# Query projections by seven block products in layer 2, an earlier last product with v, and PSUM rings kept by hand

## The chip, the cores and the metric

The kernel runs on one core of a Trainium2 chip. All arithmetic is in fp32. The metric is device time in microseconds (us) from one launch of the whole program; the median of several runs is compared. Separate from those runs, one execution was taken by the hardware profiler, and its records are the profile that is read here.

A word on the names in the profile: PE is TensorE (matmuls), PEld its weight loads, DVE is VectorE, ACT is ScalarE, POOL is GpSimd, SP is SyncE, which only issues DMA transfers here. "SPq", "ACTq" and "POOLq" are the queues on which these engines issue transfers. A line number such as L192 is a line of the kernel's file.

## The reference

The input x holds 4 images of 512 channels and 32x32 pixels, so 1024 positions ("tokens") each. Four residual layers follow one another, each behind a group norm over 32 groups:

```python
x = x + L0(gn(x))   # attention, 8 heads; scores mixed over heads, softmax, instance norm, product with v, projection
x = x + L1(gn(x))   # channel means -> a small simulated quantum circuit -> one gate per channel
x = x + L2(gn(x))   # attention, 8 heads of 64 channels
x = x + L3(gn(x))   # 2048 memory items: scores, the 8 best, softmax over them, weighted sum of the items
```

The change is mostly in layer 2:

```python
q = conv1x1(x, Wq, bq)                       # 512x512 weights on 512x1024
k, v = conv1x1(x, Wkv, bkv)                  # two more of the same size
attn = softmax(einsum('bhct,bhcs->bhts', q, k) * SCALE)      # SCALE = 1/8
out = conv1x1(einsum('bhts,bhcs->bhct', attn, v), Wp, bp)
```

## The kernel before, in words

Channels lie on the 128 partitions in KC = 4 chunks, tokens along the free dimension in two halves of NB = 512. A full 1x1 convolution is 32 matmuls of 128x512, and each fp32 matmul is two records in the profile. [...]the kernel uses three *pairs* of banks as a ring (`pairs`) and two single banks (`pv_bank`, `pt_bank`).

**Order.** TensorE executes in program order, and `pin` (L56) keeps the order in which the program writes the instructions for all that are wrapped in it. So the order of the work is written out by hand: a loop calls generators a step at a time, and each step issues a few instructions for several engines. Instructions without `pin` are placed by the framework's scheduler.

**Head.** `first()` (L294) loads image 0 in four chunks and the weights `w_q` in four chunks, alternately, on SP's queue; the parameter vectors (`gamma`, `beta`, `bproj` ...) are loaded before it on ACT's queue. For every chunk, DVE takes statistics (`stats`, L308), two tiny matmuls with `gavg` and a chain on POOL, ACT and DVE make the group's mean and deviation (`means`, `deviations`), DVE scales the chunk (`normalize`, L324), and `multiply` (L330) adds the chunk's share of the first q projection. The completion of a DMA is counted by one of eight counters, used in turn; an instruction that would reuse a counter waits until the transfer before it on this counter is complete.

**Layers 0 and 1.** For each image b = 0..3, `step` (L1436) runs for 32 units and 7 more (`STEPS` = 32, `LAG` = 7), in which the tail of this image's attention stands beside the q projections of the next image (`piece`, in the last seven steps given the list `qs`). `apply` (L523) is the product with v for a unit; after every fourth, `take_out` (L590) lets ACT copy the bank pv to SBUF, and only then may the next `apply` begin to write the bank. After the last image come the first q, k, v projections of layer 2 (`take_q2`, `take_k2`, `take_v2`) and the output projection of layer 0 for the last image (`put_out`, L729), each in a pair whose number is the last argument.

**Layer 2.** Then the PSUM pools are closed and opened again (L1590 to 1595): a pool `ps_s` with three pairs and a pool `ps_m` with two banks, from which tiles are drawn in order. Per image there are 16 units (`UNITS2`): head pair m, half n of the queries, and half of the keys from t0. `scores2` (L1165) computes four score tiles of a unit, ACT takes their exponentials, and inside it `apply2` (L1206) does the product with v of the unit before. POOL and DVE add the exponentials over the keys (L1197 to L1202); `over_keys` (L1229) ends that sum with transposes and reductions on DVE; `invert2` (L1240) makes the sum over partitions with four small matmuls (L1251), copies and inverts it, writes it to DRAM (`r`) and reads it back to all partitions (`rb`) on SP's queue; `finish2` (L1269) multiplies the block of the product with v by it (L1277).

**The borders.** Between two images of layer 2 (after b = 0, 1, 2) the next image's q, k and v and this image's output projection are computed (L1650 to L1675): q in the plain way by `take_q2`, L1141, evacuated by DVE with bias and SCALE (L1145); then the product with v of the last unit; then k, v and, after one `scores2`, the output by `seven` (L1033). That splits both factors in 2x2 blocks and needs seven products of half-size blocks in place of eight: `SEVEN` lists the products and the blocks of the result to which each is set or added. The sums of the blocks of x (t1, t3, t4 and two made in place) come from `input_sums` (L1000) on DVE, 1.2 us each. The sums of the blocks of the weights come from `weight_sums` (L1007), five DVE instructions once per matrix at the first border; the sums in place go to DRAM and are loaded for later images, while three of them stay in SBUF (`places7`). Each product (8 records by channels) fills one pair; ACT or DVE takes it from there, and `behind` is a generator of other work (norm and gating of images) that is advanced a step at a time.

**Layer 3** draws its score tiles from the same pools (`attention`, L1326; `read`, L1400).

Of the kernel before, what the change touches and what calls it, by code (L numbers as in the profile page):

```python
# [41 lines left out]
def fast_net(ctx: ExitStack, tc: tile.TileContext, a: dict, out: bass.AP, flag: bass.AP):  # L42
# [21 lines left out]
    def chan(src, name):  # L64
        t = const.tile([P, KC], F32, tag=name, name=name)
        nc.scalar.dma_start(out=t, in_=src)
        return t

    gamma = const.tile([P, NH], F32, tag="gamma", name="gamma")
    nc.scalar.dma_start(out=gamma, in_=a["in_gamma"].partition_broadcast(P))  # L70
    beta = const.tile([P, NH], F32, tag="beta", name="beta")
    nc.scalar.dma_start(out=beta, in_=a["in_beta"].partition_broadcast(P))
    bproj = chan(a["b_proj"], "bproj")
    bq2 = chan(a["bq"], "bq2")
    bk2 = chan(a["bk"], "bk2")
    bp2 = chan(a["bp"], "bp2")
    fcb = chan(a["fc_b"], "fcb")

    fcw = const.tile([NQ, C], F32, tag="fcw", name="fcw")
    nc.scalar.dma_start(out=fcw, in_=a["fc_w"])  # L80
    qpar = const.tile([P, NL * NQ], F32, tag="qpar", name="qpar")
    nc.scalar.dma_start(out=qpar, in_=a["q_params"].partition_broadcast(P))
# [3 lines left out]
    ident = const.tile([P, P], F32, tag="ident", name="ident")  # L86
    make_identity(nc, ident)
    ones = const.tile([P, P], F32, tag="ones", name="ones")
    nc.gpsimd.memset(ones, 1.0)
# [13 lines left out]
    )  # L103
    NS = 32
# [71 lines left out]
    def place(at, name):  # L176

        return pairs[at % 3] if at is not None else ps_s.tile([P, 2, NB], F32, tag="sc", name=name)
# [115 lines left out]
    def first():  # L294
# [3 lines left out]
        w = I["w_q"] = eight_k([P, KC, C], "w_q0_0", 0)  # L298
        for k in range(KC):
            nc.sync.dma_start(out=xn[:, k, :], in_=x_v[0, :, k, :])  # L300
            nc.sync.dma_start(out=w[:, k, :], in_=a["w_q"][:, k, :])
        I["w_k"] = load_w("w_k", "w_k0_0", 1)
# [5 lines left out]
        def stats(k):  # L308
            mv = small.tile([P, 2], F32, tag="mv0", name=f"mv0_{k}")
            st = small.tile([P, 2, 6], F32, tag="bnst", name=f"st_a0_{k}")  # L310
            for i in range(2):
                pin(nc.vector.bn_stats(st[:, i, :], xn[:, k, i * NB:(i + 1) * NB]))
            pin(nc.vector.bn_aggr(mv, st.rearrange("p i s -> p (i s)")))
            parts[k] = group_coeffs_parts(mv[:, 0:1], mv[:, 1:2], f"a0_{k}")

        def means(k):
            next(parts[k])
            next(parts[k])

        def deviations(k):  # L320
            next(parts[k])
            found[k] = next(parts[k])
# [15 lines left out]
        stats(0)  # L338
        means(0)
        stats(1)  # L340
        deviations(0)
        means(1)
        normalize(0)
        for k in range(KC):
            if k + 2 < KC:
                stats(k + 2)
            multiply(k, 0)
            if k + 1 < KC:
                deviations(k + 1)
            multiply(k, 1)  # L350
            if k + 1 < KC:
                normalize(k + 1)
            if k + 2 < KC:
                means(k + 2)
# [626 lines left out]
    def load2(b):  # L981
        for key in ("Wq", "Wk", "Wv"):
            load_sums(b, key, b == 1 or key == "Wq")

    def load_sums(b, key, plain):
        w = img[b][key] = eight_k([P, KC, C], f"{key}2_{b}")
        nc.sync.dma_start(out=w, in_=a[key] if plain else w_sums[key])

    H = C // 2
    w_sums = {key: dram.tile([P, KC, C], F32, tag=f"ws_{key}", name=f"ws_{key}")  # L990
              for key in ("Wk", "Wv", "Wp")}
# [15 lines left out]
    def weight_sums(b, key):  # L1007

        w = img[b][key]
        a11, a21, a12, a22 = quarters(w, H)  # L1010
        s1, s6, s7 = places7[key]
        add7(s1, a11, a22)
        sub7(s7, a12, a22)
        add7(a12, a11, a12)
        sub7(s6, a21, a11)
        add7(a21, a21, a22)
        nc.sync.dma_start(out=w_sums[key], in_=w)

# [14 lines left out]
    def seven(b, key, src, multiply, view, block, begin, done=None):  # L1033
# [7 lines left out]
        for i, (at, uses) in enumerate(SEVEN):  # L1041
            ps = ps_s.tile([P, 2, NB], F32, tag="sc", name=f"{key}_{b}_{at}")
# [24 lines left out]
    def seven_k(b):  # L1067

        dst = img[b]["k"] = big("k", f"k2_{b}")

        def begin(i, j, ps):
            for m in range(2 * i, 2 * i + 2):
                pin(nc.scalar.activation(
                    dst[:, m, j * NB:(j + 1) * NB], ps[:, m % 2, :],
                    AF.Identity, bias=bk2[:, m:m + 1]))

        return seven(b, "Wk", img[b]["xn"], by_channels, lambda ps: ps,
# [63 lines left out]
    def take_q2(b, m, at=None):  # L1141
        I = img[b]
        if m == 0:
            I["q"] = big("q", f"q2_{b}")
        project(I["Wq"], tokens(I["xn"]), m, at, lambda ps: pin(nc.vector.tensor_scalar(  # L1145
            I["q"][:, m, :], ps, bq2[:, m:m + 1], SCALE, ALU.add, ALU.mult)), f"q2_{b}")
# [18 lines left out]
    def scores2(b, u, before=None):  # L1165
# [8 lines left out]
        def exp2():  # L1174
            e = places2[:, count[0] % 6]
            count[0] += 1
            pin(nc.scalar.activation(e, scs[len(es)], AF.Exp))  # L1177
            es.append(e)

        for i, t in enumerate(range(t0, t0 + 4)):  # L1180
            sc = ps_s.tile([P, 2, NB], F32, tag="sc", name=f"sc_{nm}_{t}")
# [21 lines left out]
        if t0 == TC - 4:  # L1203
            over_keys(b, m, n)

    def apply2(b, u, exp2=None):  # L1206
# [3 lines left out]
        if t0 == 0:  # L1210
            invert2(b)
            I["pv", m, n] = ps_m.tile([P, NB], F32, tag="mm", name=f"pv_c{b}_{m}_{n}")
# [27 lines left out]
    def invert2(b):  # L1240
# [7 lines left out]
        ps = ps_s.tile([P, 2, NB], F32, tag="sc", name=f"rs_{nm}")[:, 0, 0:NS]  # L1248
# [77 lines left out]
    def attention(b, tt, between=None):  # L1326
# [3 lines left out]
        for i, (lo, hi) in enumerate(  # L1330
                ((0, T), (T, T + NB), (T + NB, NI)) if (b, tt) == tiles[-1] else ((0, T), (T, NI))):
            sc = ps_s.tile([P, T], F32, tag="sc", name=f"at_{nm}_{i}")
# [54 lines left out]
    def read_last(b, tt, picked, dg):  # L1387

        got, et, rs, xr = picked
        tp = ps_m.tile([P, KC, P], F32, tag="mm", name=f"stp_{b}_{tt}")  # L1390
# [9 lines left out]
    def read(b, tt, picked):  # L1400
# [9 lines left out]
        tp = ps_m.tile([P, KC, P], F32, tag="mm", name=f"stp_{nm}")  # L1410
# [25 lines left out]
    def step(b, s, mid, piece):  # L1436
# [35 lines left out]
        if tiled:  # L1472
            apply(b, s - LAG)
        if not tiled or s >= STEPS:
# [6 lines left out]
        if tiled and part == 3:  # L1481
# [58 lines left out]
    for b in range(B):  # L1540
# [27 lines left out]
        for m in range(KC):  # L1568
            ks[m](m + 1)
# [9 lines left out]
        if last:  # L1579
# [5 lines left out]
            for i in range(TC // 2):  # L1585
                take_v2(0, i, i + 2)
            for m in range(KC):
                put_out(b, m, m)

    stage.close()  # L1590
    pairs.clear()
    by_scalar.append(True)
    stage = ctx.enter_context(ExitStack())
    ps_s = stage.enter_context(tc.tile_pool(name="ps_s2", bufs=3, space=PSUM))
    ps_m = stage.enter_context(tc.tile_pool(name="ps_m2", bufs=2, space=PSUM))

    def small_ps(name):
        return ps_s.tile([P, 2 * NB], F32, tag="sc", name=name)
# [19 lines left out]
    for i, key in enumerate(("Wk", "Wv", "Wp")):  # L1618
        places7[key] = nine[3 * i:3 * i + 3]
    nc.gpsimd.tensor_scalar_mul(same, same, 8.0 / T)  # L1620
# [3 lines left out]
    for b in range(B):  # L1624
# [6 lines left out]
        for s, u in enumerate(UNITS2):  # L1631
# [4 lines left out]
            if s >= 1:  # L1636
                scores2(b, u, UNITS2[s - 1])
            for _ in range(2):
                if s >= 3 and last:
                    next(behind, None)  # L1640
                if s >= 8:
                    next(ahead, None)
        run_out(ahead)
        if last:
            apply2(b, UNITS2[-1])
# [4 lines left out]
        early, later = input_sums(img[b + 1]["xn"])  # L1650
        for m in range(KC):
            take_q2(b + 1, m)
            if m < 3:
                early[m]()
            if b == 0 and m < 2:
                weight_sums(1, ("Wk", "Wv")[m])
            next(behind, None)
        load_sums(b, "Wp", b == 0)
        apply2(b, UNITS2[-1])
        for i, _ in enumerate(seven_k(b + 1)):  # L1660
            if i == 0:
                invert2(b)
                for fn in later:
                    fn()
            if i == 4 and b == 0:
                weight_sums(0, "Wp")
            next(behind, None)
        finish2(b)
        early, later = input_sums(img[b]["o"])
        for i, _ in enumerate(seven_v(b + 1)):  # L1670
            if 2 <= i < 5:
                early[i - 2]()
            elif i >= 5:
                later[i - 5]()
            next(behind, None)  # L1675
        run_out(behind)
        scores2(b + 1, UNITS2[0])
        seven_out(b)

    def check_range():  # L1680
# [3 lines left out]
        tps = ps_m.tile([P, NB], F32, tag="mm", name="tot")  # L1684
# [748 lines left out]
```

## Time and profile before

| | us |
|---|---|
| median of 3 runs | 2556.93 (2554.43 to 2558.5) |
| the profiled execution | 2558.39 |
| its span, first to last instruction | 2556.6 |

The profiled execution lies 1.79 us over its span, and it is the slowest but one of the four executions.

The stretches that the change touches, each with its busy time in us and the number of instructions in brackets:

| stretch (us from the start) | length | PE busy | DVE busy | ACT busy | POOL busy |
|---|---|---|---|---|---|
| 0 to 20, head | 20.0 | 10.42 (27) | 8.22 | 1.28 | 6.18 |
| 20 to 330, first image of layer 0 | 310.0 | 297.46 (3415) | 200.13 | 146.75 | 140.78 |
| 1262 to 1275, start of layer 2 | 13.0 | 10.68 (43) | 3.24 | 4.91 | 2.78 |
| 1382 to 1500, first border | 118.0 | 115.80 (377) | 76.94 | 16.75 | 20.12 |
| 1606 to 1725, second border | 119.0 | 118.75 (374) | 72.35 | 19.02 | 15.03 |
| 1825 to 1945, third border | 120.0 | 119.75 (378) | 73.33 | 19.88 | 15.16 |

How to read it: a stretch in which PE's busy time equals its length leaves nothing to fetch but the matmuls themselves. What is missing is time in which TensorE stood still. Busy times of different engines overlap and are not to be added.

### The profile page before, as it was taken

The numbers are of one execution on the slowest core, as the hardware profiler recorded it, in microseconds if no ns is written. First come the engines' busy times: TensorE is split into PE (matmuls) and PEld (weight loads), VectorE is DVE, ScalarE is ACT, GpSimd is POOL, SyncE is SP. The second block draws the span as 40 slices with busy tenths as digits, with TensorE's granted clock in tenths as the row PEclk, the third lists the DMA queues.
The fourth block names the chain that finished last, engine by engine and source line by source line (L and its number), as shares of the span: only waits on it lengthen the run. The fifth ranks groups of instructions, "written<-read, shape, count | busy, mean of one in ns | idle before, by whom it ended". The sixth has DMA issues, their size and how long they took to land.

```text
span 2556.6 us, 47828 instructions
## 1 busy us (share of the span) xinstructions
PE 2503.3 (98%) x18534; PEld 1180.8 (46%) x18534; DVE 1685.8 (66%) x2785; ACT 985.8 (39%) x1177; POOL 1192.5 (47%) x1700
## 2 busy tenths in 40 slices
PE   8999999999999999999999999999999999999998
PEld 3344534554355534555633533453353344444445
DVE  4599448872688438881267567576657648788875
ACT  1467336651666336651153145125314612121211
POOL 3266415553465425553074147117405617566655
PEclk9999999999999999999999999999999999999999
DMA  2578438872698428982301130121014046767665
GB/s 83 145 207 237 125 120 226 244 211 74 172 243 235 131 82 211 244 248 101 124 16 55 70 112 18 54 83 59 21 54 148 18 130 190 219 186 217 187 184 170
DMA packets 187211, 361.39 MB, mean 141 GB/s; under 512 B 32729, under 2 KB 96217, under 8 KB 182882
## 3 DMA queue, kind: packets, MB, share of 16 engines
q1 hardware_dynamic: 105744, 178.71, 22.6%
q0 software_dynamic: 49152, 142.79, 20.6%
q10 hardware_dynamic: 32082, 36.76, 5.3%
q8 instruction: 149, 2.44, 0.4%
q14 instruction: 84, 0.69, 0.1%
HBM read 186.96 MB, written 36.96 MB: 88 GB/s over the span
## 4 chain that ended last, share of the span: by engine, by line
PE 74%; issue 10%; POOL 7%; DVE 3%; ACT 3%; DMA 2%; POOLq 0%; SPq 0%; ACTq 0%; DVEq 0%
PE pair L192 10%; PE sc_c L1183 9%; PE pv_c L1220 9%; PE pv L532 8%; POOL got L1360 7%; PE pair L467 6%; PE pair L493 5%; PE pt L425 5%; PE pt L721 4%; PE q L192 3%; PE Wk L1056 3%; PE Wv L1063 3%; ACT e L500 2%; PE Wp L1056 2%; PE at L1335 2%
## 5 line engine op out<-in xcount | busy, mean ns | idle before, releaser
L482 POOL DMA_DIRECT2D s<-ss x512 | 258.2, 511 | 399.5 <-PE pair L493 113.4
L506 DVE STREAM_TRANSPOSE eT<-e 128x1024 f32<-128x1024 f32 x256 | 316.5, 1236 | 193.6 <-ACT e L500 193.0
L1360 POOL DMA_INDIRECT got<-in_mem,ix x256 | 279.5, 1092 | 213.2 <-issue 122.1
L1177 ACT ACTIVATE eT<-sc_c 128x1024 f32<-128x1024 f32 x256 | 248.0, 1022 | 330.7 <-PE sc_c L1183 204.8
L521 DVE BATCH_NORM_STATS2 st<-e 128x6 f32<-128x256 f32 x1024 | 350.7, 404 | 0.0
L500 ACT ACTIVATE e<-pair 128x1024 f32<-128x1024 f32 x256 | 250.7, 1022 | 167.5 <-PE pair L493 137.2
L1201 POOL TENSOR_TENSOR e<-eT 128x1024 f32<-128x1024 f32 x96 | 232.3, 2421 | 168.6 <-DVE out L1125 69.5
L467 PE MATMUL pair<-k,q 64*32 64x512 f32 x4096 | 267.4, 598 | 12.7 <-ACT e L500 12.7
L473 ACT COPY ss<-pair 128x1024 f32<-128x1024 f32 x256 | 247.3, 1020 | 77.5 <-DMA s<-ss 37.9
L532 PE MATMUL pv<-eT,v 128*64 128x128 f32 x4096 | 250.7, 276 | 8.9 <-ACT pv L592 8.9
L532 PEld LDWEIGHTS pv<-eT,v 128*64 128x64 f32 x4096 | 221.1, 137 | 76.7 <-issue 54.5
L1183 PE MATMUL sc_c<-q,k 64*128 64x512 f32 x1024 | 240.9, 607 | 3.1 <-DVE xr L684 2.3
L1220 PE MATMUL pv_c<-eT,v 128*64 128x512 f32 x1024 | 233.0, 597 | 0.0
L1202 DVE TENSOR_TENSOR eT<-eT,e 128x1024 f32<-128x1024 f32 x96 | 136.3, 1420 | 146.3 <-POOL e L1201 146.1
L1197 POOL TENSOR_TENSOR eT<-eT 128x1024 f32<-128x1024 f32 x32 | 77.8, 2433 | 206.8 <-ACT eT L1177 202.8
L1407 DVE SCALAR_TENSOR_TENSOR acc<-got,et,acc 128x512 f32<-128x512 f32 x210 | 157.9, 752 | 7.5
L493 PE MATMUL pair<-s,wmix 32*32 32x512 f32 x4096 | 160.6, 600 | 2.3 <-issue 2.1
L1183 PEld LDWEIGHTS sc_c<-q,k 64*128 64x128 f32 x1024 | 93.6, 187 | 141.0 <-issue 71.9
L1340 ACT COPY att<-at 128x1024 f32<-128x1024 f32 (+1 forms) x65 | 64.9, 999 | 219.7 <-PE at L1335 212.9
L467 PEld LDWEIGHTS pair<-k,q 64*32 64x32 f32 x4096 | 57.0, 105 | 179.9 <-ACT e L500 86.2
L1220 PEld LDWEIGHTS pv_c<-eT,v 128*64 128x64 f32 x1024 | 68.0, 137 | 136.8 <-issue 136.8
L1335 PE MATMUL at<-memT,xn_d 128*128 128x512 f32 x256 | 120.7, 594 | 0.0
(335 smaller groups left out, 3431.3 us busy)
## 6 DMA issues: line engine op xcount, KB each, us to landing
s<-ss SPq DMA_DIRECT2D x512, 128.0 KB
s<-ss POOLq DMA_DIRECT2D x512, 128.0 KB
rb<-r POOLq DMA_DIRECT2D x64, 128.0 KB
o<-o SPq DMA_DIRECT2D x32, 256.0 KB
xr<-in_x ACTq DMA_DIRECT2D x32, 256.0 KB
x<-xr SPq DMA_DIRECT2D x32, 256.0 KB
xr_c<-x SPq DMA_DIRECT2D x32, 256.0 KB
rb_c<-r SPq DMA_DIRECT2D x64, 128.0 KB
```

The source lines that it names most:

```text
L192: pin(nc.tensor.matmul(ps[:, n, :], w[:, k, m * P:(m + 1) * P], rhs(k, n), start=(k == 0), stop=(k == KC - 1),))
L467: pin(nc.tensor.matmul(sc[m * NS:(m + 1) * NS, r, :], q[r * HD:(r + 1) * HD, m, s * NS:(s + 1) * NS], k_[r * HD:(r + 1) * HD, m, n * NB:(n ...
L482: pin(relays[side].dma_start(out=s2[2 * m + r::NH], in_=ss[m * NS:(m + 1) * NS, r, :]))
L493: pin(nc.tensor.matmul(mixed(s, r // 2)[t * NS:(t + 1) * NS, r % 2, :].rearrange("p (qq k) -> p qq k", qq=2), wmix[r * NS:(r + 1) * NS], s ...
L500: pin(nc.scalar.activation(e[:, half].rearrange("p r qq k -> p (r qq k)"), flat2(mixed(s, half)), AF.Exp))
L506: pin(nc.vector.transpose(eT[:, j % 2].rearrange("p b (qq i r) x -> p i r qq b x", qq=2, i=4)[:, i, 2 * half:2 * half + 2], e[:, half].rea ...
L521: pin(nc.vector.bn_stats(st[:, i, 2 * half + r, qq, :], e[:, half, r, qq, :]))
L532: pin(nc.tensor.matmul(pv[r * HD:(r + 1) * HD, gp, :], I["v"][:, t, g * HD:(g + 1) * HD], eT[:, j % 2, t, :, 4 * g:4 * g + 4], start=(t == ...
L1177: pin(nc.scalar.activation(e, scs[len(es)], AF.Exp))
L1183: pin(nc.tensor.matmul(sc[:, r, :], I["k"][r * HD:(r + 1) * HD, m, t * P:(t + 1) * P], I["q"][r * HD:(r + 1) * HD, m, n * NB:(n + 1) * NB] ...
L1220: pin(nc.tensor.matmul(pv[r * HD:(r + 1) * HD, :], I["v"][:, t, h * HD:(h + 1) * HD], e[:, r, :], start=(t == 0), stop=(t == TC - 1),))
L1360: pin(nc.gpsimd.indirect_dma_start(out=got[:, i, :], out_offset=None, in_=a["mem"], in_offset=bass.IndirectOffsetOnAxis(ap=ix[:, i:i + 1], ...
```

## The change

- The parameter loads are collected in a list and issued by `first` after the loads of x and w_q; chunk 0 of x comes in two halves; the chunks' group means move from POOL to DVE; 17 matmuls of ones (128x128) are put before and between the first small matmuls; statistics and scaling of the first chunks change places on DVE.
- In `step`, for the steps beyond `STEPS`, `take_out` comes before `piece`.
- At the start of layer 2 the pools are not reopened. `next_pair` and `next_bank` hand out the three pairs and the two banks in turn; k, v and the output projection at that place use pairs shifted by one or two. In a border, small matmuls use the bank that is idle (`at_border`).
- q at the borders goes by seven products. Its weight sums are made in units 10 to 14 of image 0 and stored; because three of them share a place with those of Wp, they are stored too (`w_more`) and loaded again for later images. SCALE is applied in the exponential. t1 is made in the last unit but one; t4 and t3 before q; `over_keys` of the last unit is called after them (of its DVE instructions only the second reduction ends up behind them).
- The last product with v comes ahead of q; `invert2` of the last heads stands at the fifth product of q, `finish2` at the second product of k, behind the load of Wp.
- `ahead` (statistics and norm for the next image) is advanced from unit 7 on, not 8.

The diff, cut to its core:

```diff
 
-    def chan(src, name):
-        t = const.tile([P, KC], F32, tag=name, name=name)
-        nc.scalar.dma_start(out=t, in_=src)
+    later = []
+
+    def held(shape, name, src):
...
         w = I["w_q"] = eight_k([P, KC, C], "w_q0_0", 0)
+        for n in range(2):
+            nc.sync.dma_start(out=xn[:, 0, n * NB:(n + 1) * NB], in_=x_v[0, :, 0, n * NB:(n + 1) * NB])
         for k in range(KC):
-            nc.sync.dma_start(out=xn[:, k, :], in_=x_v[0, :, k, :])
+            if k > 0:
+                nc.sync.dma_start(out=xn[:, k, :], in_=x_v[0, :, k, :])
             nc.sync.dma_start(out=w[:, k, :], in_=a["w_q"][:, k, :])
+        for load in later:
+            load()
         I["w_k"] = load_w("w_k", "w_k0_0", 1)
...
+            mv = parts[k][0]
+            ps = small_ps(f"gps_a0_{k}")
+            pin(nc.tensor.matmul(ps[:, 0:1], gavg, mv[:, 0:1], start=True, stop=True))
+            dm, sq, gm = (column(name, k) for name in ("dm", "gsq", "gm"))
+            pin(nc.vector.tensor_sub(dm, mv[:, 0:1], ps[:, 0:1]))
+            pin(nc.vector.scalar_tensor_tensor(sq, dm, dm, mv[:, 1:2], ALU.mult, ALU.add))
+            pin(nc.vector.tensor_copy(gm, ps[:, 0:1]))
...
+        def warm(times):
+            for _ in range(times):
+                pin(nc.tensor.matmul(pairs[2][:, 0, 0:P], ones, ones, start=True, stop=True))
...
-        stats(0)
+        warm(11)
+        for i in range(2):
+            stats(0, i)
-        stats(1)
+        stats(1, 0)
+        warm(2)
+        stats(1, 1)
+        warm(2)
+        normalize(0)
-        normalize(0)
+        warm(2)
-                stats(k + 2)
+                for i in range(2):
+                    stats(k + 2, i)
...
-            load_sums(b, key, b == 1 or key == "Wq")
+            load_sums(b, key, b == 1)
...
+        if not plain and key in w_more:
+            for i in range(3):
+                nc.sync.dma_start(out=places7[key][i], in_=w_more[key][:, i])
...
-              for key in ("Wk", "Wv", "Wp")}
+              for key in ("Wq", "Wk", "Wv", "Wp")}
+    w_more = {key: dram.tile([P, 3, 2, H], F32, tag=f"wm_{key}", name=f"wm_{key}")
+              for key in ("Wq", "Wp")}
...
-        add7(s1, a11, a22)
-        sub7(s7, a12, a22)
-        add7(a12, a11, a12)
-        sub7(s6, a21, a11)
-        add7(a21, a21, a22)
+        for fn, out, x, y in (
+                (add7, s1, a11, a22), (sub7, s7, a12, a22), (add7, a12, a11, a12),
+                (sub7, s6, a21, a11), (add7, a21, a21, a22)):
+            fn(out, x, y)
+            yield
...
+        if key in w_more:
+            for i in range(3):
+                nc.sync.dma_start(out=w_more[key][:, i], in_=places7[key][i])
...
-    def seven_k(b):
-        dst = img[b]["k"] = big("k", f"k2_{b}")
+    def seven_by_channels(b, name, bias):
+        dst = img[b][name] = big(name, f"{name}2_{b}")
...
-                    AF.Identity, bias=bk2[:, m:m + 1]))
-        return seven(b, "Wk", img[b]["xn"], by_channels, lambda ps: ps,
+                    AF.Identity, bias=bias[:, m:m + 1]))
+        return seven(b, "W" + name, img[b]["xn"], by_channels, lambda ps: ps,
...
-            I["q"][:, m, :], ps, bq2[:, m:m + 1], SCALE, ALU.add, ALU.mult)), f"q2_{b}")
+            I["q"][:, m, :], ps, bq2[:, m:m + 1], None, ALU.add)), f"q2_{b}")
...
-            pin(nc.scalar.activation(e, scs[len(es)], AF.Exp))
+            pin(nc.scalar.activation(e, scs[len(es)], AF.Exp, scale=SCALE))
...
-            sc = ps_s.tile([P, 2, NB], F32, tag="sc", name=f"sc_{nm}_{t}")
+            sc = next_pair()
...
-            I["pv", m, n] = ps_m.tile([P, NB], F32, tag="mm", name=f"pv_c{b}_{m}_{n}")
+            I["pv", m, n] = next_bank()
...
-        ps = ps_s.tile([P, 2, NB], F32, tag="sc", name=f"rs_{nm}")[:, 0, 0:NS]
+        ps = small_ps(f"rs_{nm}")[:, 0:NS]
...
             apply(b, s - LAG)
+        if s >= STEPS and tiled and part == 3:
+            take_out(b, j)
         if not tiled or s >= STEPS:
...
-        if tiled and part == 3:
+        if tiled and part == 3 and s < STEPS:
...
-            ks[m](m + 1)
+            ks[m](m + 1 + last)
...
-                take_v2(0, i, i + 2)
+                take_v2(0, i, i + 1)
...
-                put_out(b, m, m)
-    stage.close()
-    pairs.clear()
+                put_out(b, m, m + 2)
...
-    stage = ctx.enter_context(ExitStack())
-    ps_s = stage.enter_context(tc.tile_pool(name="ps_s2", bufs=3, space=PSUM))
-    ps_m = stage.enter_context(tc.tile_pool(name="ps_m2", bufs=2, space=PSUM))
+    turns = [0, 0]
+    def next_pair():
+        turns[0] += 1
+        return pairs[(turns[0] - 1) % 3]
+    def next_bank():
+        turns[1] += 1
+        return (pv_bank, pt_bank)[turns[1] % 2]
+    at_border = [False]
...
-        return ps_s.tile([P, 2 * NB], F32, tag="sc", name=name)
+        return (pv_bank, pt_bank)[(turns[1] + 1) % 2] if at_border[0] else flat2(next_pair())
...
-                scores2(b, u, UNITS2[s - 1])
+                scores2(b, u, UNITS2[s - 1], last or u != UNITS2[-1])
...
-                if s >= 8:
+                if s >= 7:
...
+            if s == 9 and b == 0:
+                weights = weight_sums(1, "Wq")
+            if s >= 10 and b == 0:
+                next(weights, None)
+            if s == len(UNITS2) - 2 and not last:
+                run_out(ahead)
+                first7, rest7 = input_sums(img[b + 1]["xn"])
+                first7[0]()
...
+        apply2(b, UNITS2[-1])
...
-            apply2(b, UNITS2[-1])
...
-        early, later = input_sums(img[b + 1]["xn"])
-        for m in range(KC):
-            take_q2(b + 1, m)
-            if m < 3:
-                early[m]()
-            if b == 0 and m < 2:
-                weight_sums(1, ("Wk", "Wv")[m])
+        first7[1]()
+        first7[2]()
+        over_keys(b, *UNITS2[-1][:2])
+        at_border[0] = True
+        for i, _ in enumerate(seven_by_channels(b + 1, "q", bq2)):
+            if 1 <= i < 3:
+                rest7[i - 1]()
+            if i == 4:
+                invert2(b)
+            if i == 5 and b == 0:
+                run_out(weight_sums(1, "Wk"))
...
-        apply2(b, UNITS2[-1])
-        for i, _ in enumerate(seven_k(b + 1)):
-            if i == 0:
-                invert2(b)
-                for fn in later:
-                    fn()
-            if i == 4 and b == 0:
-                weight_sums(0, "Wp")
+        for i, _ in enumerate(seven_by_channels(b + 1, "k", bk2)):
+            if i == 1:
+                finish2(b)
+            if b == 0 and i == 2:
+                run_out(weight_sums(1, "Wv"))
+            if b == 0 and i == 4:
+                run_out(weight_sums(0, "Wp"))
...
-        finish2(b)
-        early, later = input_sums(img[b]["o"])
+        first7, rest7 = input_sums(img[b]["o"])
...
-                early[i - 2]()
+                first7[i - 2]()
...
-                later[i - 5]()
+                rest7[i - 5]()
...
+        at_border[0] = False
```

## The prediction, made before the changed kernel was run

> **What bounds the kernel now.** I read four views, in this order: the busy shares, the groups by line with what ended the idle time before them, the chain of waits, and the timeline at the places that the diff touches.
>
> ```profile
> span 2556.6 us, 47828 instructions
> PE 2503.3 (98%) x18534; PEld 1180.8 (46%) x18534; DVE 1685.8 (66%) x2785; ACT 985.8 (39%) x1177; POOL 1192.5 (47%) x1700
> PE 74%; issue 10%; POOL 7%; DVE 3%; ACT 3%; DMA 2%; POOLq 0%; SPq 0%; ACTq 0%; DVEq 0%
> PE pv L532 <- ACT pv L592: 8.9, 15, 1.6
> PE sc_c L1183 <- DVE xr L684: 2.3, 1, 2.3
> PE Wk L1056 <- ACT k L1073: 2.0, 1, 2.0
> ```
>
> TensorE is busy 98% of the span at a granted clock of 0.998. The three last lines are its waits (waiting group, releaser, total us, count, longest us). So only fewer matmul records or shorter TensorE gaps move the end; a change to DVE, ACT or a queue counts if TensorE then waits. All the gaps in TensorE's timeline add up to 46.5 us, 9.6 of it in the head.
>
> The places concerned (start, us, engine, line, tiles; the brackets give idle time before and its releaser):
>
> ```profile
> 295.00 1.01 ACT L292 COPY q<-pair 128x1024 f32<-128x1024 f32 x1 [6.86 <-PE pair L192]
> 295.91 0.59 ACT L592 COPY pv<-pv 128x512 f32<-128x512 f32 x1
> 296.55 1.97 PE L532 MATMUL pv<-eT,v 128*64 128x128 f32 x32 [1.59 <-ACT pv L592]
> ...
> 1382.34 27.73 PE L192 MATMUL q<-xn_c,Wq 128*128 128x512 f32 x64
> 1410.00 3.65 PE L1220 MATMUL pv_c<-eT,v 128*64 128x512 f32 x16
> 1413.58 3.70 PE L1056 MATMUL Wk<-sums,eT 128*128 128x512 f32 x8
> ...
> 1605.31 1.23 DVE L1202 TENSOR_TENSOR eT<-eT,e 128x1024 f32<-128x1024 f32 x1 [2.54 <-POOL e L1201]
> 1605.70 3.05 POOL L1201 TENSOR_TENSOR e<-eT 128x1024 f32<-128x1024 f32 x1 [0.42 <-ACT eT L1177]
> 1606.97 2.05 DVE L1260 SCALAR_TENSOR_TENSOR seen<-ri_c,seen 128x32 f32<-128x32 f32 x2
> 1608.94 1.22 DVE L1202 TENSOR_TENSOR eT<-eT,e 128x1024 f32<-128x1024 f32 x1
> 1612.57 0.68 DVE L1277 TENSOR_TENSOR eT<-pv_c,rb_c 128x512 f32<-128x512 f32 x1
> ...
> 1410.10 0.33 SPq L987 DMA_DIRECT2D Wp<-in_Wp  x1
> 1420.48 0.32 SPq L1262 DMA_DIRECT2D r<-ris  x1
> 1425.30 0.69 DVE L1277 TENSOR_TENSOR eT<-pv_c,rb_c 128x512 f32<-128x512 f32 x1 [0.54 <-DMA rb_c<-r]
> ```
>
> See first that ACT's copy of pv, which TensorE needs, stands behind its copy of q; then how a border between images runs q, last product with v, k back to back; then that DVE is late at its start: POOL's sum holds it up, and the block product L1277 comes 6.5 us after q began.
>
> [...]the `seen` operations beside POOL's sum took 2.05 us for two; L1202 takes 1.22 us alone and 3.40 at 1591.18, while POOL sums. [...]the first four 128x512 records took 3.78 us, the next four 1.96. [...]no row of before shows a small transfer beside a 1 MB one closely enough to price it, which is why case D below stays open.
>
> **The change, part by part** (at TensorE; minus is shorter).
>
> *Head, 0.* Seventeen 128x128 warm-up matmuls go first, 11 of them before the first statistics. A cold record of this width takes 0.213 us in the tail (32 records), so 22 of them are 4.7 us, over before 11.31, when the first real matmul starts. [...]worth up to 1.9 us (3.78 against 1.87 warm) if nothing else is late. But the second chunk is: its matmuls start at 17.04 because chunk 2 of x lands only at 13.78 and 3.1 us of statistics, group means and scaling follow; and chunk 2's issue waits on SP behind the second chunk of w_q, which waits 6.1 us for a DMA counter that `bproj` holds. In the new program the parameter loads keep their order on ACT's queue and the counters are still shared in turn, so this wait only moves to the second chunk of x (for `gamma`) and of w_q. Faster first matmuls then only make a longer wait for the second. Bounds −1.5 (chunk 2 earlier too) and +1.2 (it lands later, or first scaling ends at 12.6).
>
> *pv copied ahead of q at each image's end, −4.5.* Three gaps: 1.59 at 296.55, then 1.47 and 1.47 at the two next images (583.2, 873.6): 4.53. Each ends with the 0.59 copy that stands behind q's 1.01. pv is complete at 287.8, so its copy now lies beside the 7.13 us of projection matmuls. The q copy starts up to 0.6 later; its pair is next needed after another pair's 3.46, which hides it.
>
> *Start of layer 2, −1.9.* `sc_c` waited 2.32 us at 1267.48 because the PSUM pools were closed and reopened: the first scores needed the last output tile drained by DVE. Now they take the next pair of a ring that goes on; the third pair is still that of a late drain, for which I leave an estimate of 0.4, half way between nothing and one such drain (L684 took 0.73).
>
> *q by seven products, −3.46 a border.* 7x4 = 28 matmuls are 56 records where 32 were 64 (64 took 27.73, so 0.4325 each): −8 x 0.4325 = −3.46, three times −10.4. It adds work off TensorE: 8 ACT activations 128x512 and 8 DVE additions 128x1024 of 1.22 in place of four evacuations of 1.28, some 5 us of DVE per border; five weight sums of 0.69 once, spread over units 10 to 14 of image 0; and three 256 KB reloads per border. DVE is idle for 4 to 5 us between q's evacuations (before 1620.35, 4.67), so the additions fit, except at the start:
>
> *The sums of x stand in DVE's queue ahead of q, +2.0 a border.* Product two needs t4. In DVE's order stand ahead of it t1 (1.22), the last additions over keys, reciprocal, `seen`, two key transposes, one reduction, the block product (needs `rb`), t4; only the second reduction moves behind. The addition at 1608.94 comes some 1.1 later, as t1 goes into a queue already late: 1610.0; plus 1.22, 1.30 for the transposes and 0.62 for a reduction (before: two transposes 1.30 at 1610.19, two reductions 1.24 at 1611.42): 1613.2. `rb` is there then (in before 5.45 after the reciprocal at 1606.46, so 1613.0). Plus 0.68 for the block product and 1.22 for t4: 1615.1. TensorE wants it after the product with v and product one: 1606.08 + 3.57 + 3.46 = 1613.1. Wait about 2.0. Bounds 0 (`rb` returns earlier, in the 4.8 of the other border) and 5[...]. In the first border two more weight sums (2x0.69) and a shared small bank (0.5) come on top: 3.2 + 0.5.
>
> *The first border's wait before k, −1.96.* Wk waited for ACT at 1419.80 since the small row-sum matmuls took a pair of the ring. They now go to the idle bank; the wait goes and nothing else is late there: the ring turns every 3.46, and ACT's two activations take 1.2.
>
> *Reciprocals of the last heads at product five of q; Wp loaded ahead of their broadcast.* Cost nothing, with slack of 2 us: say q's last product ends at T. SP then issues the 1 MB Wp load, which kept the DMA busy to 1414.4 (4.3 us), and behind it `r` and `rb`; those took 4.8 (issue 1420.48 to product 1425.30). `rb` is there at T+9.4. The block product stands in DVE ahead of the additions that free the ring; product five of k needs a pair at T+13.8, so `rb` by T+11.6. Each us beyond that costs one.
>
> Sum: 0 − 4.5 − 1.9 + (−3.46 −1.96 + 3.7 = −1.7) + 2 x (−3.46 + 2.0 = −1.45) = −11.0. The profiled execution took 2558.39 us, 1.8 over its span; 2547.4 in its terms. It is 1.46 over the median of the runs shown, 2556.93, so on that footing 2546.
>
> **The rivals.**
> *B, the border waits are hidden:* DVE reaches t4 in time. For it: the key sums of the last unit move behind it. Against: `rb` alone takes 5.45. Then −4.5 − 1.9 − (3 x 3.46 + 1.96 − 0.5) = −18.2, to 2539.
> *C, the borders give nearly nothing:* waits of about 4.5 us eat the 3.46. For it: L1202 at 3.40 beside POOL. Then −4.5 − 1.9 with +1.5 or so from the borders and head, −5: 2552.
> *D, slower: the Wp load on SP.* With its reloads beside it and the transfers of norm and gating, load and broadcast take twice as long: 0.3 + 8.6 + 9.6 = T+18.5, 6.9 late, while DVE stands at the block product. 3 x 6.9 − 11.0 = +9.7: 2566. It decides from 5.4 us of stall per border. For it: one queue, 1 MB ahead of 4 KB. Against: in before, `rb` lands in 4.8 with the same neighbours.
> *E, the head does not do what it says:* the parameter loads are still ahead on ACT's queue. That is in my 0 already.
>
> **How the numbers follow.** Forecast 0.59, B 0.18, C 0.15, D 0.08. What a measurement of this kernel can tell from no change is 0.2%, 5.1 us: faster is under 2551.8. Faster takes the forecast (less 0.03), B, and 0.04 of C: 0.78; same has the rest of C and of the forecast, 0.14; slower is D, 0.08. The range leaves out D and a little at each end: 2537 (B with the head's gain) to 2553 (C).
>
> **What would show it.** Right: no pv wait near 296, 583 and 874; q's records in a border 56; a gap of 1 to 3 us before the second product of q, released by DVE's sum; none before product five of k. The head's multiplications of chunk 1 still start at about 17. Wrong: gaps in a border over 4 us, or any wait in k for DVE behind `rb<-r`; or none at all in q (then B).

## The result, and the profile after

The changed kernel takes 2567.29 us (median of 6 runs, 2563.32 to 2569.29) where the kernel before took 2556.26 beside it. The ratio is 1.0041, with a 95% interval of 1.0029 to 1.0053: 11 us slower, where 11 us faster were forecast. The profiled execution of the changed kernel took 2565.92 us.

From the page of the changed kernel: its span, the busy times of the engines, and the shares of the chain of work that ended last:

```profile
span 2564.2 us, 47900 instructions
PE 2504.7 (98%) x18544; PEld 1182.6 (46%) x18544; DVE 1700.2 (66%) x2810; ACT 1000.8 (39%) x1201; POOL 1199.6 (47%) x1688
PE 86%; DVE 6%; DMA 3%; ACT 2%; issue 2%; POOL 1%; SPq 0%; ACTq 0%; POOLq 0%; DVEq 0%
```

The number of TensorE records fits: three borders save 24 and 17 warm-up matmuls add 34, so 18544 stand in place of 18534. But the busy time of TensorE did not fall, although the 24 that went are 128x512 (10.4 us) and the 34 that came took 6.5. The mean granted clock (the share of TensorE's full clock that the profile records) fell instead, from 0.998 to 0.993. A record at a lower clock counts as busy all the same (16 records of the second border, below, count 9.85 us where they take 7.13 at a clock of 1.00), so a stretch in which TensorE is busy throughout can still hold time to win. Then four lines of TensorE's waits in the changed kernel (waiting group, releaser, total us, count, longest us):

```profile
PE pair L1220 <- DVE out L1027: 9.9, 3, 3.3
PE pair L1093 <- DVE sums L1027: 6.1, 3, 4.8
PE pt L142 <- DVE eT L1314: 5.3, 2, 2.7
PE pv L561 <- ACT pv L621: 4.3, 12, 1.0
```

The pv wait fell from 8.9 to 4.3 us and lost exactly its three late ones. The first three lines are new, 21.3 us, and all are in the borders.

Where the time went can be read from the starts of matmuls that both kernels have (us from the start; the difference is after minus before):

| matmul | before | after | difference | change since the line above |
|---|---|---|---|---|
| first scores of layer 0 | 72.98 | 73.27 | +0.29 | |
| last record of layer 0's output projection | 1264.79 | 1258.96 | −5.83 | −6.1 |
| third score tile of layer 2 | 1270.81 | 1261.56 | −9.25 | −3.4 |
| after the first border (unit 1, fourth tile) | 1498.94 | 1495.60 | −3.34 | +5.9 |
| after the second border (unit 2) | 1722.69 | 1727.61 | +4.92 | +8.3 |
| first scores of layer 3 | 2047.94 | 2059.14 | +11.20 | +6.3 |

So the changed kernel was 9.25 us ahead before layer 2's first border, more than the 6.4 forecast up to there, and the three borders, which were to give 4.6, cost 20.5. At the very end 3.6 come back: the kernel before waited 3.7 us at its last gathers in this execution and the changed one 2.1, and from 2540 to 2550 us the granted clock was 0.83 before and 1.00 after.

The second border of the changed kernel, TensorE's timeline:

```profile
1606.07 3.70 PE L1093 MATMUL pair<-sums,eT 128*128 128x512 f32 x8
1612.44 0.59 PE L142 MATMUL pt<-mv_d,gavg 128*128 128x4 f32 x2 [2.67 <-DVE eT L1314]
1613.58 9.85 PE L1093 MATMUL pair<-sums,Wq 128*128 128x512 f32 x16 [0.55 <-DVE sums L1027]
...
1713.82 2.38 PE L1220 MATMUL pair<-q,k 64*128 64x512 f32 x8
1719.50 3.79 PE L1220 MATMUL pair<-q,k 64*128 64x512 f32 x8 [3.30 <-DVE out L1027]
1723.22 4.46 PE L1257 MATMUL pt<-eT,v 128*64 128x512 f32 x16
```

There are two places. At the start of q a small matmul for a norm (L142) waits 2.67 us, and behind it product two waits 0.55 more. After the output projection, at 1719.50, the third score tile waits 3.30. And after each of these waits the matmuls themselves are slow: 16 records in 9.85 us where they take 7.13, then 8 in 3.79 and 16 in 4.46 where they take 1.99 and 3.65; the granted clock was 0.50 from 1612.25 to 1619.08 and from 1718.07 to 1724.89. The same places in the first border and in the third:

```profile
1386.33 9.13 PE L1093 MATMUL pair<-sums,Wq 128*128 128x512 f32 x16 [4.81 <-DVE sums L1027]
1494.63 1.99 PE L1220 MATMUL pair<-q,k 64*128 64x512 f32 x8 [3.30 <-DVE out L1027]
1496.55 3.65 PE L1257 MATMUL pt<-eT,v 128*64 128x512 f32 x16
...
1841.00 8.79 PE L1093 MATMUL pair<-sums,Wq 128*128 128x512 f32 x16 [0.74 <-DVE sums L1027]
1945.86 2.93 PE L1220 MATMUL pair<-q,k 64*128 64x512 f32 x8 [3.30 <-DVE out L1027]
1948.72 4.35 PE L1257 MATMUL pt<-eT,v 128*64 128x512 f32 x16
```

DVE at the start of q in the second border, still the changed kernel:

```profile
1602.73 3.38 DVE L1239 TENSOR_TENSOR eT<-eT,e 128x1024 f32<-128x1024 f32 x1 [2.27 <-POOL e L1238]
1606.03 0.34 DVE L1293 RECIPROCAL ri_c<-ri_c 128x32 f32<-128x32 f32 x1
...
1611.70 0.69 DVE L1314 TENSOR_TENSOR eT<-pt,rb_c 128x512 f32<-128x512 f32 x1 [1.75 <-DMA rb_c<-r]
1612.31 2.35 DVE L1027 TENSOR_TENSOR sums<-xn_c 128x1024 f32<-128x1024 f32 x2
```

DVE stands idle 1.75 us for `rb` at the block product (L1314), and t4 and t3 (L1027) stand behind it in DVE's order though they need nothing of it. And the same block product reads the bank into which L142 wants to write, so both waits hang on `rb`.

The second place, the scores after the output projection, in the kernel before:

```profile
1714.48 4.70 PE L1183 MATMUL sc_c<-q,k 64*128 64x512 f32 x16
```

Four score tiles in one stretch, 1.0 us longer than the 3.70 of an undisturbed unit. In the compiled program of before, tiles three and four wait for ACT: the pool gave them the pairs of tiles one and two. The trace agrees: they start at 1716.80 and 1718.05, each 0.06 us after ACT's exponential of tile one and of tile two ends. In the changed kernel the ring gives tile three the pair of the seventh output product, which DVE empties last.

### The profile page after: what moved, and what is told of

Read it like the earlier page. It is cut to its first block, busy times and chain, and to the rows that moved or that the text cites. A ratio compares the mean times of both kernels' runs of the same rounds, so it can differ in the third digit from the quotient of the medians.

```text
span 2564.2 us, 47900 instructions
## 1 busy us (share of the span) xinstructions
PE 2504.7 (98%) x18544; PEld 1182.6 (46%) x18544; DVE 1700.2 (66%) x2810; ACT 1000.8 (39%) x1201; POOL 1199.6 (47%) x1688
## 4 chain that ended last, share of the span: by engine, by line
PE 86%; DVE 6%; DMA 3%; ACT 2%; issue 2%; POOL 1%; SPq 0%; ACTq 0%; POOLq 0%; DVEq 0%
PE pair L1372 17%; PE pair L189 11%; PE pair L1220 8%; PE pv L561 8%; PE pair L1093 7%; PE pair L496 6%; PE pair L522 5%; PE pt L454 5%; PE pt L1257 4%; PE pt L750 3%; PE pv L1257 3%; PE pair L1100 3%; ACT e L529 2%; DMA s<-ss 2%; PE pair L774 1%
## 5 line engine op out<-in xcount | busy, mean ns | idle before, releaser
L1214 ACT ACTIVATE eT<-pair 128x1024 f32<-128x1024 f32 x256 | 248.0, 1022 | 355.0 <-PE pair L1220 224.0
L1238 POOL TENSOR_TENSOR e<-eT 128x1024 f32<-128x1024 f32 x96 | 237.5, 2477 | 179.4 <-ACT eT L1214 138.2
L496 PE MATMUL pair<-k,q 64*32 64x512 f32 x4096 | 267.3, 598 | 12.8 <-ACT e L529 12.6
L1220 PE MATMUL pair<-q,k 64*128 64x512 f32 x1024 | 241.7, 609 | 10.6 <-DVE out L1027 9.9
L1220 PEld LDWEIGHTS pair<-q,k 64*128 64x128 f32 x1024 | 93.2, 187 | 148.1 <-issue 69.0
L1377 ACT COPY att<-pair 128x1024 f32<-128x1024 f32 (+1 forms) x65 | 64.9, 999 | 219.4 <-PE pair L1372 219.2
L1372 PE MATMUL pair<-memT,xn_d 128*128 128x512 f32 x256 | 120.7, 594 | 0.0
L1372 PE MATMUL pair<-memT,eT 128*128 128x512 f32 x256 | 120.4, 593 | 0.0
L1372 PE MATMUL pair<-eT 128*128 128x512 f32 x256 | 120.3, 592 | 0.0
```

The costliest lines, as they stand in the source:

```text
L496: pin(nc.tensor.matmul(sc[m * NS:(m + 1) * NS, r, :], q[r * HD:(r + 1) * HD, m, s * NS:(s + 1) * NS], k_[r * HD:(r + 1) * HD, m, n * NB:(n ...
L1214: pin(nc.scalar.activation(e, scs[len(es)], AF.Exp, scale=SCALE))
L1220: pin(nc.tensor.matmul(sc[:, r, :], I["k"][r * HD:(r + 1) * HD, m, t * P:(t + 1) * P], I["q"][r * HD:(r + 1) * HD, m, n * NB:(n + 1) * NB] ...
L1372: pin(nc.tensor.matmul(sc[:, i0 - lo:i0 - lo + NB], xn3[b][:, k, tt * P:(tt + 1) * P], memT[k][:, i0:i0 + NB], start=(k == 0), stop=(k == ...
```

## The experiments

Each median stands beside runs of the kernel before on the same chip. A gain or loss against the changed kernel is the difference between the two distances from the kernel before (the changed kernel's own is 11.0 us).

**e1, the old choice of pairs after the output projection.**

```diff
+            if i == 2 and I.pop("back", False):
+                turns[0] -= 2
             sc = next_pair()
...
         seven_out(b)
+        img[b + 1]["back"] = True
```

> Only change to the changed kernel: in the first four score tiles after each output projection, the third and fourth use the pairs of the first and second again, as the pool did before; the ring goes on with the pair of the seventh output product after them. Theory (the fixed ring gives the third score tile the pair that DVE drains last): the wait of 3.30 us for DVE at that place, three times, becomes the wait of about 1.1 us for ACT that the kernel before had, and the slow records after it at the second and third border (2.7 and 1.7 us) go: 3 x 2.2 + 4.4 = 11 us less, near 2556. Rival (DVE is late there whatever the pair, so the wait only moves to the next tile): no change, 2567.

Measured 2555.70 us, ratio to before 0.9989 (0.9980 to 0.9997): 12.8 us less than the changed kernel. The trace at the second border:

```profile
1715.87 4.68 PE L1222 MATMUL pair<-q,k 64*128 64x512 f32 x16
1720.48 3.65 PE L1259 MATMUL pt<-eT,v 128*64 128x512 f32 x16
```

The 4.70 us of the kernel before are back, and the product with v behind is at full speed. The ring's choice is the cause at this place.

**e2, t4 and t3 ahead of the block product, and the small norm matmul one product later.**

```diff
         run_out(ahead)
+        if not last:
+            first7[1]()
+            first7[2]()
         apply2(b, UNITS2[-1])
...
-        first7[1]()
-        first7[2]()
         over_keys(b, *UNITS2[-1][:2])
...
-            next(behind, None)
+            if i > 0:
+                next(behind, None)
```

> Two changes to the changed kernel: the block sums t4 and t3 stand on DVE ahead of the block product that waits for rb, and the small norm matmul comes one product later, so that it does not wait for the bank that this block product reads. Theory (both waits at the start of q hang on rb, which lands 5.1 us after its issue): the gaps there, 4.81, 3.22 and 3.34 us, fall to under 1 each, and the slow records after them (2.0, 2.7, 1.7) go: 10 + 6 = 16 us less, near 2551. Rival (the added DVE work of q by seven products is what is too much; the wait moves to a later product of q or k): at most 5 us less.

Measured 2550.15 us, 0.9972 (0.9963 to 0.9982): 18.4 us less than the changed kernel. At the second border in its trace:

```profile
1605.64 3.70 PE L1093 MATMUL pair<-sums,eT 128*128 128x512 f32 x8
1609.17 3.60 PE L1093 MATMUL pair<-sums,Wq 128*128 128x512 f32 x8
1612.61 0.28 PE L142 MATMUL pt<-mv_d,gavg 128*128 128x4 f32 x2
1612.75 3.68 PE L1093 MATMUL pair<-sums,Wq 128*128 128x512 f32 x8
```

There is no gap and no slow record; at the first border 0.70 us of the 4.81 stay. The trace has no wait at a later product of q or k, so DVE's extra work is not too much.

**e5 and e6, each half of e2 alone.** e5 has the first two blocks of that diff, e6 the last.

> Of e2 only the first change: t4 and t3 ahead of the block product on DVE; the small norm matmul stays between the first and the second product of q. Theory (two waits on the same rb, one behind the other in TensorE's order): at the first border, where no norm matmul stands there, the gap of 4.81 us falls to about 1 and the 2.0 us of slow records go, 6 us; at the second and third the matmul for the norm still waits 2.6 us for its bank, and only the 0.55 and 0.74 behind it go: 7 us less than the changed kernel, near 2560. Rival (the sums alone are the cause): all of e2, near 2550.

> Of e2 only the second change: the small norm matmul one product later; t4 stays behind the block product. Theory: the second product of q still waits for t4 until the same time, 3.2 us, so nothing changes, 2567. Rival (the shared bank alone is the cause at the second and third border): 5.3 us of waits and 4.4 us of slow records go there, near 2557.

e5 measured 2561.13 us, 1.0017 (1.0010 to 1.0024), 6.8 less than the changed kernel; e6 2569.45, 1.0047 (1.0030 to 1.0064), no gain. So it is two waits on one `rb`, in series: with the sums early, L142 still waits 2.58 us at the second border; with L142 out of the way, product two waits for t4 (4.04 us in the profile of e6). Only both together give e2. The waits show this more surely than the times: in the profiles of both halves the third score tile at the first border waits 6.2 us in place of 3.30, because DVE stood for a load and its next operation took 2.5 and 2.9 us in place of 0.70. Whether the edits bring this about or chance does is not shown; with the slow records behind it, it makes the gain of each half uncertain by some 5 us.

**e3 and e9, filling the gaps.** e3 puts matmuls that nothing reads between products one and two of q; e9 puts as many ahead of the third score tile too. The question is whether the records behind a wait are slow because of the granted clock, which was 0.50 at five of the six places in the changed kernel.

```diff
+            if key == "Wq" and i == 0:
+                for _ in range(12):
+                    pin(nc.tensor.matmul(
+                        pairs[turns[0] % 3][:, 0, 0:P], ones, ones, start=True, stop=True))
             yield
```

> Added to the changed kernel: 12 matmuls of ones, 128x128, between the first and the second product of q at each border, into the pair that is free; nothing reads them. The waits stay as long as they are. Theory [...]: 2.0, 2.7 and 1.7 us of slow records go, 6.4 us less, near 2561. Rival (these records are slow because of what they read, or because DVE and POOL are busy beside them): no gain, and up to 1 us more per border where the filling is longer than the gap.

> e3, and 12 more matmuls of ones at the other wait too, ahead of the third score tile after each output projection, into the bank that the next product with v overwrites. The waits themselves stay. Theory [...]: against the changed kernel the slow records go at both places, 6.4 us at q (e3 measured 4 by the medians) and 4.4 at the scores, so 3 to 5 us less than e3, near 2559. Rival (the slow records at the scores are slow for another reason): as e3, 2563 or more.

e3 measured 2563.15 us, 1.0026 (1.0017 to 1.0036), 5.4 less than the changed kernel. e9 measured 2557.46, 1.0004 (0.9997 to 1.0010), 10.0 less. TensorE in e9 at the second border:

```profile
1609.45 2.84 PE L1090 MATMUL pair<-ones 128*128 128x128 f32 x24
1612.26 0.39 PE L142 MATMUL pt<-mv_d,gavg 128*128 128x4 f32 x2
1613.39 7.13 PE L1097 MATMUL pair<-sums,Wq 128*128 128x512 f32 x16 [0.75 <-DVE sums L1027]
...
1713.22 2.94 PE L1224 MATMUL pt<-ones 128*128 128x128 f32 x24
1716.60 1.99 PE L1229 MATMUL pair<-q,k 64*128 64x512 f32 x8 [0.43 <-DVE out L1027]
1718.52 3.65 PE L1266 MATMUL pt<-eT,v 128*64 128x512 f32 x16
```

The useful records start as late as before (product two 7.5 us after product one, the third score tile 5.7 after the first, as in the changed kernel), read the same data beside the same DVE and POOL work, and take 7.13, 1.99 and 3.65 us in place of 9.85, 3.79 and 4.46. The granted clock from 1603 to 1624 us was 0.84 in the changed kernel and 1.00 in e9, from 1711 to 1730 us 0.82 and 1.00. So what the slow records had lost was the clock. Useless work in the waits takes back nearly all that the change had lost, though not everywhere: at the first border of e9 the filling ended 2.20 us before t4 came, and the 16 records behind took 8.83 us (granted clock from 1375 to 1395 us: 0.91).

**e4, the edits of e1 and e2 together.**

> The edits of e1 and e2 together. Theory: they are separate places and add up: 11 + 16 = 27 us less than the changed kernel, near 2540, and 16 us less than the kernel before. Rival (DVE's extra work at the borders sets the time): not under 2556.

Measured 2535.27 us, 0.9920 (0.9907 to 0.9932): 33.3 us less than the changed kernel and faster than both kernels by more than 20. e1 and e2 add up (12.8 + 18.4 = 31.2). Of the three border lines only 0.7 us of one is left in its list of waits (L1093, at the first border), and its clock is 1.0. The head of that list:

```profile
PE pair L496 <- ACT e L529: 12.5, 56, 1.5
PE pv L561 <- ACT pv L621: 4.3, 12, 1.0
PE pt L326 <- DVE mv L318: 2.1, 2, 1.7
```

**e7, e4 with the plain q.**

```diff
-            if s >= 10 and b == 0:
-                next(weights, None)
...
-        for i, _ in enumerate(seven_by_channels(b + 1, "q", bq2)):
+        for m in range(KC):
+            take_q2(b + 1, m)
```

> e4 with the plain q at the borders, 32 matmuls of 128x512 in place of 28; no weight sums of Wq, and the two sums in place of x move to the first product of k. Theory (with the waits gone the seven products are worth their matmuls, 3.46 us a border): 10.4 us more than e4, near 2546. Rival (their work on DVE and ACT costs part of it elsewhere): 5 us more than e4 or less, near 2540.

Measured 2544.26 us, 0.9948 (0.9932 to 0.9965): 9.6 us more than e4, where the records alone make 10.4. The seven products are worth their 8 records a border once nothing waits.

**e8, the old place of pv's copy in the changed kernel.**

```diff
-        if s >= STEPS and tiled and part == 3:
-            take_out(b, j)
...
-        if tiled and part == 3 and s < STEPS:
+        if tiled and part == 3:
```

> The changed kernel with the copy of pv behind the copy of q again at the end of images 0 to 2. Theory: three waits of 1.5 us come back, 4.7 us more, near 2572. Rival (they were hidden by what follows): 2567.

Measured 2572.72 us, 1.0063 (1.0046 to 1.0079): 4.8 us more than the changed kernel.

**e10, e4 without the warm-up matmuls** (`warm` does nothing).

> e4 without the 17 warm-up matmuls of the head. Theory (the second chunk of the first projection waits for chunk 2 of x, at 17 us, whatever the clock before): no change from e4 within 1 us, 2535. Rival (a warm array in the first microseconds is worth its 1.9 us): 2 us more, 2537.

Measured 2538.38 us, 0.9934 (0.9921 to 0.9948). The distances from the kernel before differ by 4.2 us, but the two intervals overlap. By the time alone the rival, 2 us more, is the nearer. The first q projection, in e4 and then in e10:

```profile
10.39 1.89 PE L354 MATMUL pair<-xn_all,w_q 128*128 128x512 f32 x4
...
16.40 1.98 PE L354 MATMUL pair<-xn_all,w_q 128*128 128x512 f32 x4 [1.10 <-DVE dm_a L328]
```

```profile
10.38 3.78 PE L354 MATMUL pair<-xn_all,w_q 128*128 128x512 f32 x4
14.24 2.18 PE L354 MATMUL pair<-xn_all,w_q 128*128 128x512 f32 x4
16.40 1.96 PE L354 MATMUL pair<-xn_all,w_q 128*128 128x512 f32 x4
```

Behind the warm-up matmuls the first four records take 1.89 us in place of 3.78, and then TensorE waits; the second chunk starts at 16.40 either way, and the first scores of layer 0 at 72.37 and 72.35. The 2.3 us between these two executions arise later, between 73 and 450 us, in layer 0, which the edit leaves alone. Whether they are chance stays open; in these two executions they do not come from the head.

## Why the prediction was wrong, point by point

- **The head, forecast 0:** right, +0.29 us at the first scores. Chunk 2 of x landed late as argued (its statistics start at 14.21 against 13.78), and e10 shows the start of chunk 1's matmuls not to move.
- **pv ahead of q, forecast −4.5:** right. The wait list lost 4.6 us, and e8 gives 4.8 (the interval of each of its two ratios is some 3 to 4 us wide to either side).
- **Start of layer 2, forecast −1.9:** right in kind, too small: −3.4 from the last record of the output projection to the third score tile. The third tile still waited 0.31. The kernel before paid more than the wait of 2.32 us: from 1267.72 to 1271.13 its granted clock was 0.50, while the changed kernel kept 1.00 at this place. The sum had priced the gap and not the records behind it. Of the 6.1 us gained ahead of this place pv explains some 4.6; the rest arose in layers 0 and 1, and its cause is not shown.
- **q by seven products, −3.46 a border:** right; e7 against e4 gives 9.6 us for three.
- **The sums of x in DVE's queue, forecast waits of 3.7, 2.0 and 2.0:** the chain was right, the size was not. (By its own terms the first is 2.0 + 2 x 0.69 + 0.5 = 3.9.) Measured 4.81, 3.22 and 3.34, and 1.03 more at a product with v shortly before the first border (1356.10), which waits for its bank. At the second border the reciprocal ended at 1606.37, with q starting at 1606.07; the addition ahead of it had taken 3.38 us while POOL summed, against 1.22 alone (at 1606.83), a case that the prediction kept for its upper bound; the block product that needs `rb` began 5.3 us later. The shared bank, priced at 0.5 in the first border, holds at the second and third as well (L142), behind the same `rb`.
- **The first border's wait before k, −1.96:** right, the list of waits no longer has it.
- **`rb` behind the 1 MB load of Wp, no cost:** right, though not by the path that was forecast. At the second border the load of Wp was issued at 1630.55, 7.3 us before q's last product ended (1637.82), and not after it. The block product ran at 1639.00, 1.2 us after that end, where the prediction allowed 11.6. So rival D did not happen. That the result lies beside D's 2566 is luck: its mechanism is another.
- **What failed.** Two terms of the sum were missing, and each stood in it at nothing. The step "now they take the next pair of a ring that goes on" was looked at once, at the start of layer 2, and not where the same ring follows the output projection: it cost 3.30 us there, three times, where the pool had cost 1.0. And each wait was counted at its own length, though the prediction itself had counted slow records at the head (3.78 us for the first four, 1.96 for the next). The records behind the waits cost 2.0, 2.7 and 1.7 us at q and, scores and product with v together, 0, 2.6 and 1.6 after the output projection. These two and the longer waits at q are 3 x 2.3 + 10.6 + (12.4 − 7.7) = 22.2 of the 25 us between the borders' forecast (−4.6) and what they did (+20.5). e1 shows the ring, e2 the waits at q, and e3 and e9 the slow records; the last 3 us are not accounted for.

## What to carry to other kernels

- A pool that becomes a ring by hand changes who waits for whom at every place where the ring meets a pair that is emptied late. List, for each tile, which engine frees its buffer, before and after, and do so wherever one stage follows another.
- Price a gap in TensorE at its length plus the slow records behind it. Here the waits of 2.3 to 4.8 us had up to 2.7 us of them, though one wait of 3.30 us had none. Where a gap can't be removed, matmuls that nobody reads can keep the clock up, if they fill it (e9 at the second border: 1.00, against 0.84 and 0.82).
- When two instructions wait for the same late transfer in series, an edit to one shows nothing or little; where instructions run in the program's order (DVE stood 1.75 us for `rb` with t4 and t3 behind it), what doesn't need the transfer belongs ahead of what does. e2 gained 18.4 us by this, its halves 6.8 and nothing.

## What the runs showed of the hardware

The granted clock of the changed kernel around three of its waits, each time the 3.41 us ahead of a change of the clock and the stretch after it; the first two lines are the wait of 3.30 us at the first border, after which nothing changed (columns: stretch, length, busy time of PE, PEld, DVE, ACT, POOL with counts, granted clock, DMA share, GB/s):

```profile
1489.37:1492.79 3.42, 1.84 (x8) 0.30 (x4) 3.28 (x6) 2.05 (x2) 0.26 (x1) 1.00 1.05 407
1492.79:1496.20 3.41, 1.57 (x8) 0.69 (x8) 3.04 (x5) 0.00 (x0) 2.09 (x1) 1.00 1.05 394
1608.84:1612.25 3.41, 0.93 (x3) 0.10 (x1) 1.66 (x3) 2.42 (x4) 0.00 (x0) 1.00 0.54 153
1612.25:1619.08 6.83, 6.09 (x9) 2.90 (x10) 3.00 (x4) 0.16 (x1) 1.53 (x3) 0.50 0.26 80
1714.66:1718.07 3.41, 1.42 (x6) 0.30 (x4) 3.27 (x6) 2.05 (x2) 0.67 (x1) 1.00 1.04 389
1718.07:1724.89 6.82, 5.39 (x12) 1.71 (x14) 5.65 (x10) 0.00 (x0) 1.68 (x1) 0.50 0.65 229
```

The second border of e9, where the same waits are filled:

```profile
1603.00:1624.00 21.00, 20.25 (x74) 10.18 (x71) 14.76 (x17) 5.17 (x10) 5.47 (x7) 1.00 0.19 52
1711.00:1730.00 19.00, 18.45 (x92) 7.98 (x94) 13.37 (x20) 7.87 (x8) 8.13 (x4) 1.00 0.78 286
```

In the kernel before, TensorE waited 2.32 us, up to 1267.48, and the granted clock was 0.50 from 1267.72 to 1271.13; in the changed kernel it waited 2.67 and 0.55 us around a tiny matmul, up to 1612.44 and 1613.58, and the clock was 0.50 from 1612.25 to 1619.08. In the changed kernel's borders the 0.50 lasted 3.41 us (from 1840.95 and 1946.76) or 6.83 us (from 1383.56, 1612.25 and 1718.07). It is not a matter of length alone: of three waits of 3.30 us after the output projection the first was followed by 8 records in 1.99 us, at a granted clock of 1.00, and the others by 3.79 and 2.93, at 0.50 from 1718.07 and from 1946.76.

From one of these five places of the changed kernel to the next the clock's falls lie 228.69, 105.82, 122.88 and 105.81 us apart, which is 67, 31, 36 and 31 times 3.413. TensorE stood for 2.0 us of the 3.41 ahead of 1718.07 and for 2.5 ahead of 1946.76. At the first of the three waits it stood for 1.6 us in the stretch of 3.42 up to 1492.79 and for 1.84 in the next 3.41, and the clock stayed at 1.00. Why the clock fell after some waits and not after others is not shown.
